# Deformable convolution, attention and experts: the first image's gather table made ahead of its offsets

## The chip, the core and the metric

The kernel runs on one core of one Trainium2 chip, in one launch. The time is device time in microseconds (us); the number that counts is the median of several runs. The profile is one further execution, recorded instruction by instruction. Engines: PE multiplies matrices (PEld loads its stationary operand), DVE is the vector engine, ACT the scalar engine, POOL (GpSimd) issues the indirect transfers, SP issues the other transfers.

## What is computed

Two layers over an image batch x of shape (4, 256, 64, 64). The change lies in the first, a modulated deformable 3x3 convolution over group-normalized x, added to x:

```python
    om = conv(gn(x), w_off) + b_off            # 27 channels: 18 offsets, 9 mask logits
    off = om[:, :2 * K2].reshape(B, K2, 2, Ho, Wo)
    mask = jax.nn.sigmoid(om[:, 2 * K2:])
    ys = off[:, :, 0] + hs[None, None, :, None] + (ki * DIL)[None, :, None, None]
    xs = off[:, :, 1] + ws[None, None, None, :] + (kj * DIL)[None, :, None, None]
    sampled = jax.vmap(_bilinear)(x, ys, xs)   # four corners, zero outside of the image
    sampled = sampled * mask[:, None]
    out = jnp.einsum('bckhw,ock->bohw', sampled, w_conv.reshape(O, C, K2))
```

The second layer is a token-wise attention between the four images (tied over positions) and a mixture of 8 experts, of which each token takes 2. Its code isn't touched, apart from the place of three small loads.

## The kernel before

**Sampling.** Each image has 32 tiles of 128 positions, and each tile 9 taps: 288 steps an image, 1152 in all, in one loop whose order of instructions on PE, DVE, ACT and POOL is written out by hand (L601 `tc.manual_schedule`); SP's order is left to a scheduler. A step gathers, for 128 positions, a row of 1024 numbers (the four corners of the tap, 256 channels each) from a table in DRAM (L519). ACT multiplies corner 0 by its weight (L535), DVE adds the other three (L543), PE transposes the sum (L557), ACT copies it out (L563), and PE multiplies it by the tap's convolution weights into an accumulator (L582). Ten gather buffers are in turn: the gather for step n + 10 waits for the last corner of step n.

**The table.** For each image b, `tables[b]` holds at each padded position two neighbouring rows' channels; a gathered row is two such entries. Its borders are zeros; `borders`-like stores (L262 to L266, five for each image) write them for all four images at the start. The inside comes from `block(q)`, eight blocks of 512 positions: `norm` makes xs, the normalized block (L353, ACT, one for each half of the channels), `turn` transposes it on PE (L363), `leave` copies it out on ACT (L372) and stores it with four transfers on SP (L378). Two zt buffers are in turn.

**The offsets.** The same `block(q)` makes the 27 offset channels from xs: `rows_of` (six products into po, L390), `shifted` (three shifted copies on ACT into oc, L402), `summed` (four small products into pt, L411), `kept` (a copy on DVE into om, L417). po, pt and the small statistics pm share two PSUM buffers (tag "om" of `ps_om`), tpx and tps the four of `ps_tp`. When all eight blocks are there, sixteen DVE operations on 576 or 288 elements a partition (L452 to L488) and a sigmoid on ACT (L447) turn om into the gather's indices idx and the corner weights wts.

**Where this stands in time.** `pieces(b)` lists all of that, with the step at which each piece is to be issued: the group statistics from step 32 (16 pieces), block q of 25 steps at 56 + 22 q, positions from step 235. For images 1 to 3 the pieces stand between the sampling steps of the image before. For image 0 there is nothing to stand between: `emit(pieces(0))` runs them at the start, in an order that the scheduler picks, and `routed` after them (L136 to L152), which multiplies the router's weights into the convolution's weights on PE and copies 18 small results on DVE. The first gather comes after all of this. `load_image(b + 1)` (L223) comes at the first step for image 1, and six steps before the end of an image for the others.

Of the kernel before, what the change touches and what calls it, by code (L numbers as in the profile page):

```python
# [9 lines left out]
F32 = mybir.dt.float32  # L10
I32 = mybir.dt.int32
AF = mybir.ActivationFunctionType
ALU = mybir.AluOpType
# [28 lines left out]
LOAD_AHEAD = 6  # L42
FIRST = 32
PERIOD = 22
NBLK = HW // BLK
# [24 lines left out]
def conv_attn_moe_kernel(  # L70
# [50 lines left out]
    def per_channel(ap, name):  # L121
# [3 lines left out]
        return t  # L125

    gamma_c = per_channel(gamma, "gamma_c")
    beta_c = per_channel(beta, "beta_c")
    bg_c = per_channel(bg, "bg_c")

# [71 lines left out]
    with ExitStack() as actx:  # L202
# [44 lines left out]

        ocs = [aw.tile([3 * QUAD, RB, W], F32, name=f"oc{n}") for n in range(2)]
        for oc in ocs:
# [6 lines left out]

        zeros = aw.tile([P, 4 * C], F32, name="zeros")
        G.memset(zeros, 0.0)
        for b in range(B):
            tv = tables[b].rearrange("(y x) (two c) -> y x two c", x=TW, two=2)  # L260
            zv = zeros.rearrange("p (a two c) -> p a two c", a=2, two=2)
            nc.sync.dma_start(tv[0, 1 : W + 1, 0, :], zeros[:W, :C])  # L262
            nc.sync.dma_start(tv[H, 1 : W + 1, 1, :], zeros[:W, :C])
            nc.sync.dma_start(tv[H + 1], zv[:TW, 0])
            nc.sync.dma_start(tv[: H + 1, 0], zv[: H + 1, 0])
            nc.sync.dma_start(tv[: H + 1, W + 1 :], zv[: H + 1])  # L266

# [16 lines left out]

        params = {}

        def pieces(b):


            out_ = []  # L290
            xr = xraw[b]
# [26 lines left out]

            n = FIRST
            for ch in range(NCH):  # L320
                for j in range(NBLK):
                    out_.append((n, lambda ch=ch, j=j: stats(ch, j)))
                    n += 1
# [11 lines left out]
            tv = tables[b].rearrange("(y x) (two c) -> y x two c", x=TW, two=2)  # L335
            om = atmp.tile([P, NR, NOFF], F32, name=f"om{b}", tag="om")

            def block(q):

                y0 = q * RB - 1  # L340
                lo, hi = max(y0, 0), min(y0 + RB + 2, H)
                t = {}

                def norm(ch):
                    if ch == 0:
                        t["xs"] = apad.tile(
                            [P, NCH, RB + 2, W], F32, name=f"xs{b}_{q}", tag="xs"
                        )
                        if lo > y0:
                            G.memset(t["xs"][:, :, 0, :], 0.0)  # L350
                        if hi < y0 + RB + 2:
                            G.memset(t["xs"][:, :, RB + 1, :], 0.0)
                    S.activation(  # L353
                        t["xs"][:, ch, lo - y0 : hi - y0], xrv[:, ch, lo:hi], AF.Identity,
                        bias=nb[:, ch : ch + 1], scale=rs[:, ch : ch + 1],
                    )

# [10 lines left out]
                def leave(i):  # L368
                    if i == 0:
                        t["zt"] = ast.tile([P, NT, C], F32, name=f"zt{b}_{q}", tag="zt")  # L370
                    zt = t["zt"]
                    S.copy(zt[:, i, :], t["tp"])  # L372
                    if i < NT - 1:
                        return
                    for yl in range(2):
                        for two in range(2):
                            yy = q * RB + yl + 1 - two
                            nc.sync.dma_start(  # L378
                                tv[yy : yy + RB - 1 : 2, 1 : W + 1, two, :].rearrange(
                                    "t x c -> x t c"  # L380
                                ),
                                zt[yl * W : (yl + 1) * W],
                            )
# [11 lines left out]

                oc = ocs[q % 2]

# [18 lines left out]
                def kept():  # L416
                    V.tensor_copy(om[:, q * NT : (q + 1) * NT, :], t["pt"])  # L417

                at = n + q * PERIOD
                out_.append((at, lambda: norm(0)))  # L420
                out_.append((at + 1, lambda: norm(1)))
                for i in range(NT):
                    out_.append((at + 3 + 4 * i, lambda i=i: turn(i)))
                    out_.append((at + 4 + 4 * i, lambda i=i: leave(i)))
                for m in range(NCH * 3):
                    out_.append((at + 4 + 2 * m + m // 2, lambda m=m: rows_of(m)))
                for kj in range(3):
                    out_.append((at + 18 + kj, lambda kj=kj: shifted(kj)))
                out_.append((at + 22, lambda: summed(0)))
                out_.append((at + 23, lambda: summed(1)))  # L430
                out_.append((at + 24, kept))

            for q in range(NBLK):
                block(q)
            n += (NBLK - 1) * PERIOD + 25

            shape = [P, 2, NR, K2]
            t = {}  # L440

            def tmp(key, tag, dtype=F32, shape=shape):
                t[key] = atmp.tile(shape, dtype, name=f"{key}{b}", tag=tag)
                return t[key]

            def masked():
                S.activation(  # L447
                    tmp("mask", "mask", shape=[P, NR, K2]), om[:, :, 2 * K2 :], AF.Sigmoid
                )

            def placed():
                V.tensor_tensor(  # L452
                    tmp("pos", "pos"),
                    om[:, :, : 2 * K2].rearrange("p r (k two) -> p two r k", two=2),
                    grid, ALU.add,
                )

            def indexed():
                p0 = t["p0"]
                params[b] = [ap_.tile([P, NR, K2], I32, name=f"idx{b}", tag="idx")]  # L460
                V.tensor_scalar(
                    p0[:, 0], p0[:, 0], float(TW), float(TW + 1), ALU.mult, ALU.add
                )
                V.tensor_tensor(params[b][0], p0[:, 0], p0[:, 1], ALU.add)

            def weighted(corner):


                if corner == 0:
                    params[b].append(  # L470
                        ap_.tile([P, 4, NR, K2], F32, name=f"wts{b}", tag="wts")
                    )
                wy, wx = (("hi", "lo")[corner % 2], ("hi", "lo")[corner // 2])
                V.tensor_tensor(params[b][1][:, corner], t[wy][:, 0], t[wx][:, 1], ALU.mult)

            def both(key):
                V.tensor_tensor(t[key][:, 0], t[key][:, 0], t["mask"], ALU.mult)

            for fn in (
                placed,  # L480
                lambda: V.tensor_tensor(t["pos"], t["pos"], taps, ALU.add),
                lambda: V.tensor_scalar(t["pos"], t["pos"], -1.0, float(H), ALU.max, ALU.min),
                lambda: V.tensor_copy(tmp("pi", "ki32", I32), t["pos"]),
                lambda: V.tensor_copy(tmp("p0", "p0"), t["pi"]),
                lambda: V.tensor_tensor(tmp("over", "over"), t["p0"], t["pos"], ALU.is_gt),
                lambda: V.tensor_tensor(t["p0"], t["p0"], t["over"], ALU.subtract),
                lambda: V.tensor_tensor(tmp("lo", "over"), t["pos"], t["p0"], ALU.subtract),
                lambda: V.tensor_scalar(  # L488
                    tmp("hi", "pos"), t["lo"], -1.0, 1.0, ALU.mult, ALU.add
                ),  # L490
                indexed,
                lambda: both("hi"),
                lambda: both("lo"),
                *(lambda c=c: weighted(c) for c in range(4)),
            ):
                out_.append((n, fn))
                n += 1
            out_.append((n - 15, masked))
            assert n <= STEPS - AHEAD, n
            return out_  # L500

        def emit(todo):
            for _, fn in sorted(todo, key=lambda p: p[0]):
                fn()
# [89 lines left out]

        emit(pieces(0))
        routed(
# [4 lines left out]
        with tc.manual_schedule(engines=order):  # L601
# [5 lines left out]
            for n in range(2):  # L607
                corners(n)
            todo = {}
            for n in range(total + 2):  # L610
                b, at = divmod(n + LOAD_AHEAD, STEPS)
                if at == 0 or n == 0:
                    if b + 1 < B:
                        load_image(b + 1)
                        for when, fn in pieces(b + 1):
                            todo.setdefault(b * STEPS + when, []).append(fn)
# [86 lines left out]

    rsum = route_pool.tile([P, NE], F32, name="rsum")

    with ExitStack() as bctx:
# [782 lines left out]
```

## Time and profile before

| what | us |
|---|---|
| median of three runs (3273.08, 3274.14, 3282.42) | 3274.14 |
| the profiled execution, time | 3278.02 |
| the profiled execution, span of its instructions | 3276.3 |
| opening, up to the first gather (L519) | 127.8 |
| sampling, first gather to the last step's products | 127.8 to 1863.7 |
| attention and experts after it | 1863.7 to 3276.3 |

Over the whole span PE is busy for 2972.6 us (91%), DVE 2600.0 (79%), POOL 1854.4 (57%), ACT 1722.3 (53%). A busy PE isn't PE at its peak, since its instructions are pipelined and their ends modelled; so the stretches count more than the sum. The granted PE clock was 0.958 over the span, 0.86 in the first 128 us.

Times of the four images, from the copy of an image's first accumulator (L591) to that of the next image's first: 152.9, 601.8, 1053.1 and 1492.7 us are the four starts; the last copy is at 1863.7.

How to read the page's lines: a group has its line, engine, operation, result<-operands, shape and count, then busy us and mean ns of one, then the idle time just before it and what ended that. A wait has who waited for whom, the sum, how often, and the longest.

### The profile page before, as it was taken

What the parts mean: (1) busy time and instruction counts of PE and PEld (TensorE: products, weight loads), DVE (VectorE), ACT (ScalarE), POOL (GpSimd) and SP (SyncE); (2) the same over time, 40 slices, a digit from 0 to 9 for tenths busy, and PEclk for the clock granted to TensorE, in tenths of its full rate; (3) what the DMA queues carried; (4) which work ended last, traced back from release to release, by engine and by line L of the source; (5) the groups of instructions that cost most, each with busy time, mean ns of one, the idle gap of its engine ahead of it and who ended that gap; (6) DMA issues with size and microseconds to landing.
All of it is one profiled execution on the core that took longest, in us unless ns stands there. A gap on an engine that the chain in (4) does not pass through costs nothing. (4 is left out here: it accounts for less than half of the span.)

```text
span 3276.3 us, 49563 instructions
## 1 busy us (share of the span) xinstructions
PE 2972.6 (91%) x13658; PEld 2175.3 (66%) x13658; DVE 2600.0 (79%) x6611; ACT 1722.3 (53%) x3912; POOL 1854.4 (57%) x1800
## 2 busy tenths in 40 slices
PE   6889998899998899989999898978888899999995
PEld 2667776677776677767777644434444488888883
DVE  1488888878897888899999788878888766567777
ACT  3456665556664566655555444334242355556552
POOL 0377667676676767677777411105676767554440
PEclk8799999999998999999999899989999999999995
DMA  5789999999999899999999821106453445447778
GB/s 167 261 330 405 390 386 345 400 340 386 390 351 393 336 402 386 386 342 409 409 404 402 312 66 55 60 24 200 156 173 104 136 137 169 159 159 248 245 236 316
DMA packets 322182, 898.89 MB, mean 274 GB/s; under 512 B 43218, under 2 KB 89949, under 8 KB 319860
## 3 DMA queue, kind: packets, MB, share of 16 engines
q0 software_dynamic: 191808, 671.74, 53.1%
q1 hardware_dynamic: 130100, 223.98, 21.1%
q8 instruction: 113, 1.85, 0.2%
q14 instruction: 161, 1.32, 0.1%
HBM read 744.43 MB, written 154.79 MB: 274 GB/s over the span
## 5 line engine op out<-in xcount | busy, mean ns | idle before, releaser
L543 DVE SCALAR_TENSOR_TENSOR s<-g,wts,s 128x256 f32<-128x256 f32 x3456 | 1446.5, 480 | 226.4 <-ACT s L535 220.2
L519 POOL DMA_INDIRECT g<-table,idx x1152 | 1220.6, 1060 | 536.7 <-DVE s L543 279.7
L582 PE MATMUL acc<-wconv_sb,sT 128*128 128x264 f32 x4608 | 1275.2, 400 | 58.6 <-ACT sT L563 57.7
L582 PEld LDWEIGHTS acc<-wconv_sb,sT 128*128 128x128 f32 x4608 | 794.2, 192 | 186.6 <-ACT sT L563 83.9
L535 ACT ACTIVATE s<-g,wts 128x256 f32<-128x256 f32 x1152 | 587.5, 510 | 342.1 <-DMA g<-table,idx 322.4
L563 ACT COPY sT<-tps 128x256 f32<-128x256 f32 x1152 | 418.8, 364 | 352.9 <-PE tps L557 347.5
L557 PE MATMUL tps<-ident,s 128*128 128x128 f32 x2304 | 449.1, 277 | 48.6 <-DVE s L543 48.0
L557 PEld LDWEIGHTS tps<-ident,s 128*128 128x128 f32 x2304 | 316.3, 144 | 260.6 <-issue 170.9
L1313 POOL DMA_INDIRECT ys_rows<-y,to x284 | 282.7, 995 | 259.6 <-DVE y L1310 191.5
L1039 POOL DMA_INDIRECT xs_rows<-u,slots x256 | 260.6, 1018 | 126.8 <-issue 110.7
L1284 PE MATMUL ph<-xT,w 128*128 128x256 f32 x1136 | 270.8, 381 | 0.7 <-ACT hT L1288 0.6
L1302 PE MATMUL py<-w,hT 128*128 128x256 f32 x1136 | 268.4, 379 | 0.0
L1288 ACT ACTIVATE hT<-ph,w 128x256 f32<-128x256 f32 x284 | 134.4, 474 | 198.0 <-PE ph L1284 197.5
L1302 PEld LDWEIGHTS py<-w,hT 128*128 128x128 f32 x1136 | 215.8, 190 | 29.3
L1307 DVE TENSOR_TENSOR y<-py,w 128x512 f32<-128x512 f32 x142 | 98.2, 692 | 171.0 <-ACT w L1246 129.8
L1284 PEld LDWEIGHTS ph<-xT,w 128*128 128x128 f32 x1136 | 206.2, 192 | 24.1 <-ACT hT L1288 1.6
L390 PE MATMUL po<-xs,woff_sb 128*96 128x512 f32 x384 | 204.3, 628 | 0.0
L176 POOL TENSOR_TENSOR l_rstd<-l_ve,nhalf 128x4 f32<-128x4 f32 x32 | 34.4, 1075 | 253.7 <-DVE l_ve L170 253.7
L881 ACT ACTIVATE gate<-pg,bg_c 128x512 f32<-128x512 f32 x64 | 43.9, 686 | 243.0 <-PE pg L686 242.9
L759 DVE SCALAR_TENSOR_TENSOR junk<-q,k 128x512 f32<-128x512 f32 x256 | 160.9, 684 | 8.9 <-ACT k L752 8.9
L876 DVE SCALAR_TENSOR_TENSOR mix<-pv,att,mix 128x512 f32<-128x512 f32 x192 | 129.7, 742 | 1.9 <-PE pv L686 1.9
L908 PE MATMUL po<-wo_sb,mix 128*128 128x264 f32 x512 | 117.8, 386 | 0.0
(228 smaller groups left out, 3287.8 us busy)
## 6 DMA issues: line engine op xcount, KB each, us to landing
xt<-xs_rows SPq DMA_DIRECT2D x142, 260.0 KB
table<-zt SPq DMA_DIRECT2D x128, 256.0 KB
early_state<-ys_rows SPq DMA_DIRECT2D x128, 256.0 KB
g<-table,idx POOLq DMA_INDIRECT x1152, 7.8
t<-o SPq DMA_DIRECT2D x32, 528.0 KB
bt<-t SPq DMA_DIRECT2D x32, 528.0 KB
dt<-t SPq DMA_DIRECT2D x64, 264.0 KB
xraw<-in_x SPq DMA_DIRECT2D x16, 1024.0 KB
```

The source lines that it names most:

```text
L390: T.matmul(t["po"], woff_sb[:, ch, ki].rearrange("p kj o -> p (kj o)"), t["xs"][:, ch, ki : ki + RB], start=(n == 0), stop=(n == NCH * 3 - 1),
L519: g = G.indirect_dma_start(out=gs[n % NGB], out_offset=None, in_=tables[b], in_offset=bass.IndirectOffsetOnAxis(ap=params[b][0][:, r, k : ...
L535: first = S.activation(ss[n], gs[n % NGB][:, :C], AF.Copy, scale=params[b][1][:, 0, r, k : k + 1])
L543: last_corner[n] = V.scalar_tensor_tensor(ss[n], gs[n % NGB][:, c * C : (c + 1) * C], params[b][1][:, c, r, k : k + 1], ss[n], ALU.mult, A ...
L557: T.transpose(tps[n][:, ch * P : (ch + 1) * P], s[:, ch * P : (ch + 1) * P], ident)
L563: S.copy(sTs[n], tps.pop(n))
L582: T.matmul(accs[n // K2][:, :CR], sT[:, ch * P : (ch + 1) * P], wconv_sb[:, ch, k, :], start=False, stop=(k == K2 - 1 and ch == NCH - 1),)
L759: V.scalar_tensor_tensor(junk, qs[s_][:, ch, :], 1.0, ks[t_][:, ch, :], ALU.mult, ALU.mult, accum_out=parts[:, ch, s_ * B + t_, j : j + 1],)
L1039: s = G.indirect_dma_start(out=rows_, out_offset=bass.IndirectOffsetOnAxis(ap=slots[:, k, n : n + 1], axis=0), in_=u[:, n % NT, :], in_off ...
L1284: T.matmul(ph, w1_sb[:, ch, f * P : (f + 1) * P], xT[:, ch, :], start=(ch == 0), stop=(ch == NCH - 1),)
L1302: T.matmul(py[:, i, :], hT[:, f, i * P : (i + 1) * P], w2_sb[:, f, :], start=(f == 0), stop=(f == NCH - 1),)
L1313: s = G.indirect_dma_start(out=ys_rows[g], out_offset=bass.IndirectOffsetOnAxis(ap=to[:, i : i + 1], axis=0), in_=y[:, i, :], in_offset=No ...
```

## The change

- Image 0's blocks come at the start without most of their offsets: all eight write the table, and only the first three (EARLY = 3) make offsets there and positions block by block. Their norms are made by DVE (`alone=True`) instead of ACT.
- Offsets and positions of blocks 3 to 7 become pieces between the sampling steps of image 0, at steps (q - 2) * 36 + 12: 48, 84, 120, 156 and 192. For these, xs is normalized a second time (ACT, a tag and buffer of its own), and oc has a third tile. Two position operations are issued in each step, on 72 or 36 elements instead of 576 or 288.
- The borders of tables 1 to 3 are stored together with the load of their image, and these loads wait for the last table store of the image before in SP's order (`issue_after`). The zero tile is half as wide; the widest border store reads it twice.
- gamma, beta and bg are loaded later.
- For images 1 to 3 the pieces are the ones of before, at the same steps.

```diff
+EARLY = 3
...
-    gamma_c = per_channel(gamma, "gamma_c")
-    beta_c = per_channel(beta, "beta_c")
-    bg_c = per_channel(bg, "bg_c")
...
-        ocs = [aw.tile([3 * QUAD, RB, W], F32, name=f"oc{n}") for n in range(2)]
+        ocs = [aw.tile([3 * QUAD, RB, W], F32, name=f"oc{n}") for n in range(3)]
...
-        for b in range(B):
+
+        def borders(b):
...
-            nc.sync.dma_start(tv[: H + 1, W + 1 :], zv[: H + 1])
+            nc.sync.dma_start(
+                tv[: H + 1, W + 1 :], zv[: H + 1].to_broadcast([H + 1, 2, 2, C])
+            )
...
-            def block(q):
-
+            def block(q, at, table=True, offsets=True, alone=False):
...
-                    S.activation(
-                        t["xs"][:, ch, lo - y0 : hi - y0], xrv[:, ch, lo:hi], AF.Identity,
-                        bias=nb[:, ch : ch + 1], scale=rs[:, ch : ch + 1],
-                    )
+                    to, of = t["xs"][:, ch, lo - y0 : hi - y0], xrv[:, ch, lo:hi]
+                    scale, bias = rs[:, ch : ch + 1], nb[:, ch : ch + 1]
+                    if alone:
+                        V.tensor_scalar(to, of, scale, bias, ALU.mult, ALU.add)
+                    else:
+                        S.activation(to, of, AF.Identity, bias=bias, scale=scale)
...
-                            nc.sync.dma_start(
+                            stores[b] = nc.sync.dma_start(
...
-                oc = ocs[q % 2]
+                oc = ocs[q % 2 if table else 2]
...
+            def positions(rows, given, at, each):
...
+                for i, fn in enumerate((
+                    placed,
+                    lambda: add(t["pos"], taps[:, :, rows]),
+                    clamp,
+                    lambda: V.tensor_copy(tmp("pi", "ki32", I32), t["pos"]),
+                    lambda: V.tensor_copy(tmp("p0", "p0"), t["pi"]),
+                    compare,
+                    lambda: V.tensor_tensor(t["p0"], t["p0"], t["over"], ALU.subtract),
+                    rest,
+                    other,
+                    indexed,
+                    lambda: both("hi"),
+                    lambda: both("lo"),
+                    *(lambda c=c: weighted(c) for c in range(4)),
+                )):
+                    done_.append((at + i // each, fn))
+                done_.append((at + 1, masked))
+                return done_
...
+            if b:
+                for q in range(NBLK):
+                    block(q, n + q * PERIOD)
...
+            place_for()
             for q in range(NBLK):
-                block(q)
...
+                early = q < EARLY
+                later_ = block(q, n + 6 * q, offsets=early, alone=True)
+                if early:
+                    later_.extend(
+                        positions(rows_in(q), lambda q=q: of[q], n + 17 * q + 25, 1)
+                    )
+                first.extend(later_)
+            for q in range(EARLY, NBLK):
+                at = (q - 2) * NT * K2 + 12
+                block(q, at, table=False)
+                later.extend(positions(rows_in(q), lambda q=q: of[q], at + 25, 2))
+                assert at + 33 <= q * NT * K2 - AHEAD, q
+            emit(first)
+            return later
...
-        emit(pieces(0))
+        borders(0)
+        todo = {}
+        for when, fn in pieces(0):
+            todo.setdefault(when, []).append(fn)
...
-                        load_image(b + 1)
+                        with tc.issue_after(stores[b].ins):
+                            load_image(b + 1)
+                            borders(b + 1)
```

## The prediction

> **What bounds the kernel now.** First the windows, to see which engine is full in which stretch (columns: stretch and its length, busy us and count of PE, PEld, DVE, ACT, POOL, granted PE clock, DMA share, GB/s).
>
> ```profile
> 30.00:80.00 50.00, 40.73 (x127) 19.23 (x125) 1.08 (x4) 21.80 (x39) 0.00 (x0) 0.83 0.45 118
> 112.00:126.00 14.00, 13.95 (x72) 13.85 (x70) 2.30 (x5) 3.72 (x10) 0.00 (x0) 0.50 0.43 173
> ...
> 251.00:497.00 246.00, 244.23 (x1290) 190.51 (x1289) 202.64 (x493) 165.79 (x410) 166.62 (x165) 1.00 1.01 393
> 1500.00:1660.00 160.00, 154.41 (x802) 122.46 (x800) 152.30 (x360) 95.91 (x253) 115.51 (x121) 1.00 1.02 408
> ```
>
> In the opening (30 to 80) nothing but PE works much. In the middle of image 0 (251 to 497), where the blocks of image 1 are made between the steps, PE is full: 244.23 of 246. In image 3, which makes no blocks (1500 to 1660), DMA and DVE are full. Then the steps in each of the two (corner 0 runs once a step):
>
> ```profile
> L535 ACT ACTIVATE s<-g,wts 128x256 f32<-128x256 f32 x162 | 82.8, 511 | 5.9 <-DMA g<-table,idx 3.4 <-DVE s L543 2.0
> L535 ACT ACTIVATE s<-g,wts 128x256 f32<-128x256 f32 x120 | 61.0, 509 | 64.4 <-DMA g<-table,idx 62.3 <-DVE s L543 2.1
> ```
>
> So 246/162 = 1.52 us a step with blocks; without them 1.28 us, the distance of two neighbouring corners in the timeline (149.66, 150.94, 152.22). Last the waits of the opening, and its timeline:
>
> ```profile
> POOL g L519 <- DVE idx L464: 39.0, 1, 39.0
> DVE wconv_sb L152 <- PE wconv_pr L147: 11.6, 1, 11.6
> PE wo_tp L143 <- DMA wo_sb<-in_wo: 2.4, 1, 2.4
> ```
>
> ```profile
> 23.29 0.16 DVE L317 SCALAR_TENSOR_TENSOR nb<-gm,rs 128x2 f32<-128x2 f32 x1 [0.84 <-POOL rs L329]
> 96.75 1.04 PE L363 MATMUL tpx<-ident,xs 128*128 128x128 f32 x8
> 99.02 1.20 ACT L372 COPY zt<-tpx 128x256 f32<-128x256 f32 x4
> 99.05 1.07 PE L411 MATMUL pt<-tap_sum,oc 96*128 96x27 f32 x8 [1.27 <-ACT oc L402]
> 99.96 5.37 PE L390 MATMUL po<-xs,woff_sb 128*96 128x512 f32 x12
> 100.25 3.43 SPq L378 DMA_DIRECT2D table<-zt  x4
> 103.73 4.43 SPq L223 DMA_DIRECT2D xraw<-in_x  x4
> 125.98 0.17 DVE L152 COPY wconv_sb<-wconv_pr 128x8 f32<-128x8 f32 x1 [11.59 <-PE wconv_pr L147]
> 127.77 1.51 POOL L519 DMA_INDIRECT g<-table,idx  x1 [38.98 <-DVE idx L464]
> ```
>
> The first gather goes at 127.77, held by the indices; the indices were held by one router copy that stood ahead of them on DVE and waited 11.59 us for PE. The table's last store was issued by 103.7.
>
> **The change, part by part.** All sums are made against the profiled execution (3278.02 us, span 3276.3). The median of the runs, 3274.14, lies 3.9 lower; I take those 3.9 off at the end.
>
> *The first gather.* It now waits for the table's last store, since only the indices of blocks 0 to 2 are made ahead of it and no router copy stands before them on DVE. When does that store land? The three per-channel loads leave the head of SP (image load at 2.32 now, at 0.80 then), so the group statistics end at 23.45 - 1.5 = 21.9. PE then has, up to the end of block 0's offsets, 18 offset products (two passes each; 12 passes 5.37, so 0.43 a pass, 0.86 a product) = 15.5, 25 transposes of 1.04/8 = 3.3, four sums 1.1: 19.9 at full clock, 24 at the 0.83 of the opening, and some 3 more for the half-rate start: 49. Block 2's offsets leave PE about 3 later: 52. Behind them DVE has 45 operations on 36 or 72 elements and six norms. The small ones aren't in the trace; neighbours are 0.16 (128x2) and 0.76 (128x576, two tensors): I take 0.23, ends 0.16 and 0.35. A norm of 128x640 with two scalars per partition isn't there either: L188, the same operation on 128x256, takes 0.409, which scales to 0.73 to 0.8 back to back; the low end is L482, 0.452 for 128x576 with constants.
>
> ```profile
> L188 DVE TENSOR_SCALAR bt<-bt,l_mv,l_rstd 128x256 f32<-128x256 f32 x20 | 7.0, 409 | 5.1 <-POOL l_rstd L176 5.1
> L482 DVE TENSOR_SCALAR pos<-pos 128x576 f32<-128x576 f32 x3 | 1.4, 452 | 0.0
> ```
>
> 45 x 0.23 + 6 x 0.73 = 14.7, so DVE is done at 67; last transposes and copies 2.2, then the stores of blocks 6 and 7 one after the other on SP, 3.43 each, 75 to 76; the stores issued from 58.74 to 62.16 kept DMA busy until 65, so landing takes 3 more: 78 at best. Two store buffers, each free only when its store has landed, can add a few us to each of the last blocks; if PE stays at half clock it is 90. I take 81, ends 78 and 92: 127.8 - 81 = **-46.8** (-50 to -36).
>
> [...]
>
> *The router products of the convolution's weights* (18 rounds of 1.17 us, 105 to 126) stay behind the last transposes on PE, from about 71 to 92 now, and DVE's first corner behind them. They hide under the gathers: see the next term. [...]
>
> *Given back at once.* Image 1's load (4 x 1024 KB) and one table's borders (652 KB) went before the first gather; now they are issued right behind the last store. 4.86 MB at the 408 GB/s of the full window are 11.9 us; some 4 pass before the first gather's packets, **+8** (+4 to +12) on gathers that pace at 1.28. Queued on SP behind them is only the first t1 store, which nobody waits for until the next phase.
>
> *Five blocks of offsets move into image 0.* Each is 6 x 0.86 + 8 x 0.13 = 6.2 us of PE. PE is full there: 162 steps x 1.11 (distance of its transposes at 143.30, 144.41 and 145.53, where data is ready) + 18 tiles x 0.6 (image and router products, 151.69 to 152.28) + 7.4 blocks x 7.2 (8 transposes, 12 passes, 8 sums) = 244, against 244.23 busy. So they cost 5 x 6.2 = 31, less some 2.5 where the first of them (steps 48 to 56) meets image 1's statistics, where PE has idle time: **+28.5** (+20 to +33). Their other engines have cover: ACT 4 us a block at 165.79 of 246 busy, DVE some 4 at 202.64 of 246. Where a norm of one chain meets a shift of the other in one step, ACT holds sT back: **+2** (0 to +6).
>
> *Borders of tables 2 and 3* (five issues each on SP, ahead of the next image's load, some 2.5 us of SP before steps that don't need that load for 30 steps) move into steps where DMA isn't the bound, 1.6 us each at 408 GB/s: **+1** (0 to +3). *The next phase:* the moved buffers let five weight loads be issued ahead of the last gathers; the 2.4 us that wo_tp waited for its load go: **-2.4** (-3 to 0).
>
> Sum: -46.8 + 8 + 28.5 + 2 + 1 - 2.4 = -9.7: 3278.0 - 9.7 = 3268.3, and 3.9 lower for the median, **3264.4**.
>
> **Rivals.** *The added blocks don't fit between the others (slower).* Both chains take po and pt from the same two PSUM buffers and pass through ACT in order. In the opening each block made PE wait 2.23 us for its shift. If each of the five blocks stops PE twice for that, and image 1's block beside it twice, 5 x 4 x 2.23 = 45 instead of the 2 taken: 3307; with half of these stops 3285. It decides from 20 us on. For it: one po of image 1 needs a buffer that is freed in the same step; against it: PE waits for almost nothing with one chain in flight. *The gather comes late (no change):* at 92 the saving is 36, the sum +1, 3275; with none of the load over before the gathers 3279. For it: DVE makes all positions of block 2 ahead of the last two norms. *PE has room (clearly faster):* then the 28.5 fall away, 3236; 244.23 of 246 speaks against it. *That the change doesn't do what it says:* if the first gather waited for all indices, nothing would be saved; in the changed program's order of instructions the first gather waits for the queue of the stores alone, and block 0's indices stand far ahead on DVE.
>
> **How the numbers follow.** About 0.3%, 9.8 us, is what a measurement of this kernel can tell from no change. The sum holds: 0.58, with 3264 as its middle and 3256 to 3274 its own range; that is at the bound, so 0.34 faster and 0.24 the same. PE has room: 0.08, faster. Late gather: 0.17, of it 0.11 the same, 0.06 slower. Blocks don't fit: 0.17, 0.13 slower, 0.04 the same. Together 0.42, 0.39, 0.19. The range: low is the gather at 78, 4 given back, 24 for the blocks, 3 from the next phase: -49.8 + 4 + 24 - 3 = -24.8, 3249; high is the late gather with one stop of 2.23 a block, 3275 + 11 = 3286.
>
> **What would show it.** First gather at 78 to 92; steps 48 to 217 of image 0 at about 1.69 us instead of 1.52 (image 0's tiles together 30 us longer), the other images unchanged to 3 us; PE at 98% there. Wrong: a gather after 95, PE under 93% in that stretch, or image 0 longer by less than 20.

## The result, and the profile after

| | before | after |
|---|---|---|
| median of 10 runs each, us | 3274.63 | 3262.86 |
| lowest and highest | 3266.56, 3290.80 | 3253.61, 3268.85 |
| profiled execution, span | 3276.3 | 3251.8 |
| first gather | 127.77 | 78.63 |
| copy of the first accumulator of image 0 | 152.9 | 113.4 |
| images 0, 1, 2, 3 (first copy to first copy, image 3 to its last) | 448.9, 451.3, 439.6, 371.0 | 474.5, 443.8, 437.6, 371.0 |
| last accumulator copy to the end | 1412.6 | 1411.6 |

The ratio after to before, taken over the runs, is 0.9954, 95% interval 0.9934 to 0.9974: 15 us faster, between 9 and 22. The two medians lie 11.8 us apart, inside that interval. The prediction was 3264.4.

First the windows of after (columns as in the prediction: busy us and counts of PE, PEld, DVE, ACT, POOL, then granted PE clock, DMA share, GB/s), and one group of the steps in the third of them:

```profile
30.00:80.00 50.00, 36.78 (x160) 26.25 (x159) 15.46 (x66) 20.81 (x51) 1.41 (x2) 0.67 0.78 191
78.60:90.00 11.40, 11.40 (x60) 11.40 (x59) 0.00 (x0) 3.80 (x10) 8.55 (x9) 0.50 1.01 406
175.00:455.00 280.00, 276.62 (x1396) 206.34 (x1395) 217.84 (x579) 183.44 (x441) 170.53 (x171) 1.00 0.95 346
1540.00:1640.00 100.00, 95.99 (x505) 76.84 (x503) 95.02 (x226) 59.99 (x159) 72.24 (x76) 1.00 1.02 405
```

```profile
L593 ACT ACTIVATE s<-g,wts 128x256 f32<-128x256 f32 x165 | 84.2, 510 | 0.6
```

In the steps that now carry two chains of blocks, PE is busy for 276.62 of 280 us, and a step takes 280/165 = 1.70 us (before: 1.52). DMA, at a share of 1.01 in the middle of image 0 before, is down to 0.95 there, so it isn't what sets the pace. Image 3 is as it was. Then the waits of the opening, and its timeline:

```profile
DVE wconv_sb L149 <- PE wconv_pr L144: 28.4, 1, 28.4
POOL g L577 <- DMA table<-zt: 16.9, 1, 16.9
ACT zt L378 <- DMA table<-zt: 6.3, 3, 2.6
```

```profile
21.49 0.16 DVE L317 SCALAR_TENSOR_TENSOR nb<-gm,rs 128x2 f32<-128x2 f32 x1 [0.84 <-POOL rs L330]
61.49 1.07 DVE L360 TENSOR_SCALAR xs<-xraw,rs,nb 128x576 f32<-128x576 f32 x2 [1.60 <-PE tpx L369]
68.82 1.20 ACT L378 COPY zt<-tpx 128x256 f32<-128x256 f32 x4 [2.38 <-DMA table<-zt]
74.50 3.53 SPq L220 DMA_DIRECT2D xraw<-in_x  x4
78.63 1.21 POOL L577 DMA_INDIRECT g<-table,idx  x1 [16.91 <-DMA table<-zt]
79.71 9.10 SPq L263 DMA_DIRECT2D table<-zeros  x1
90.98 1.41 DVE L149 COPY wconv_sb<-wconv_pr 128x8 f32<-128x8 f32 x18 [28.42 <-PE wconv_pr L144]
91.82 0.51 ACT L593 ACTIVATE s<-g,wts 128x256 f32<-128x256 f32 x1 [2.32 <-DMA g<-table,idx]
```

The last thing that the first gather waits for is the table's last store. DVE's 18 router copies now wait 28.4 us without holding the gather; they hold DVE's first corner until 92. Behind the last store stand image 1's load and a border store whose issue takes 9.10 us.

The two profiled executions lie 24.4 us apart: that of after is the fastest of its ten runs, that of before 3.4 us above its median. Summed by stretches, the profiles give -49.1 (first gather), +9.6 (from the first gather to the first accumulator copy: 34.7 us against 25.1), +25.6 (image 0), -9.5 (images 1 and 2), -1.0 (the phases behind). Images 1 and 2 run the same instructions at the same steps in both kernels, and nearly all of the -9.5 stands in one place of each, shortly after the statistics of the next image: -7.0 between the sixth and the eighth accumulator copy of image 1, -2.4 at the same copies of image 2. The timeline of POOL, image 1, before and then after:

```profile
671.61 0.22 POOL L350 MEMSET xs<- 128x128 f32 x1
672.00 7.53 POOL L519 DMA_INDIRECT g<-table,idx  x1 [0.17 <-DVE s L543]
```

```profile
657.47 0.22 POOL L354 MEMSET xs<- 128x128 f32 x1
657.86 0.95 POOL L577 DMA_INDIRECT g<-table,idx  x1 [0.17 <-issue]
```

One gather takes 7.53 us or 0.95. From the sixth to the seventh accumulator copy of image 1, where this falls, it took 18.1 us before, 13.1 after, and 13.1, 16.7, 14.5 and 14.5 in the first four runs below: it varies between executions of the same instructions. Without images 1 and 2 the change is worth 24.4 - 9.5 = 14.9 us, close to the ratio of the runs. Image 0 has the same varying place (18.9 us before, 15.4 after), so this agreement to a few tenths is in part chance.

### The profile page after: what moved, and what is told of

It reads as the page before. It is cut to its first block, busy times and chain, and to the rows that moved or that the text cites. A ratio compares the mean times of both kernels' runs of the same rounds, so it can differ in the third digit from the quotient of the medians.

```text
span 3251.8 us, 49706 instructions
## 1 busy us (share of the span) xinstructions
PE 2965.7 (91%) x13658; PEld 2178.1 (67%) x13658; DVE 2620.5 (81%) x6747; ACT 1717.1 (53%) x3913; POOL 1829.6 (56%) x1801
## 5 line engine op out<-in xcount | busy, mean ns | idle before, releaser
L577 POOL DMA_INDIRECT g<-table,idx x1152 | 1197.3, 1039 | 563.1 <-DVE s L601 330.8
L640 PE MATMUL acc<-wconv_sb,sT 128*128 128x264 f32 x4608 | 1273.3, 399 | 54.5 <-ACT sT L621 53.2
L1368 PEld LDWEIGHTS py<-w,hT 128*128 128x128 f32 x1136 | 216.1, 190 | 29.5
L1350 PEld LDWEIGHTS ph<-xT,w 128*128 128x128 f32 x1136 | 206.7, 192 | 24.4 <-ACT hT L1354 1.7
L173 POOL TENSOR_TENSOR l_rstd<-l_ve,nhalf 128x4 f32<-128x4 f32 x32 | 34.7, 1084 | 250.8 <-DVE l_ve L167 250.8
L396 PE MATMUL po<-xs,woff_sb 128*96 128x512 f32 x324 | 166.3, 598 | 0.0
```

The source lines that it names most:

```text
L396: T.matmul(t["po"], woff_sb[:, ch, ki].rearrange("p kj o -> p (kj o)"), t["xs"][:, ch, ki : ki + RB], start=(n == 0), stop=(n == NCH * 3 - 1),
L577: g = G.indirect_dma_start(out=gs[n % NGB], out_offset=None, in_=tables[b], in_offset=bass.IndirectOffsetOnAxis(ap=params[b][0][:, r, k : ...
L640: T.matmul(accs[n // K2][:, :CR], sT[:, ch * P : (ch + 1) * P], wconv_sb[:, ch, k, :], start=False, stop=(k == K2 - 1 and ch == NCH - 1),)
L1350: T.matmul(ph, w1_sb[:, ch, f * P : (f + 1) * P], xT[:, ch, :], start=(ch == 0), stop=(ch == NCH - 1),)
L1368: T.matmul(py[:, i, :], hT[:, f, i * P : (i + 1) * P], w2_sb[:, f, :], start=(f == 0), stop=(f == NCH - 1),)
```

## The experiments

e1 to e4 ran where the kernel before had a median of 3276.88, as in the result; e5 to e8 and e9 to e12 on two other chips, where it had 3620.99 and 3622.56. There the opening is the same and the sampling is slower (see e9), so of those runs the opening is compared, and whole times only as ratios to before on the same chip. The times inside a run come from one profiled execution each. "The changed kernel" is after.

**e1: all offsets ahead of the first gather.** One part alone: table first and borders later, but no block moved.

```diff
-EARLY = 3
+EARLY = 8
```

> All eight blocks make offsets ahead of the first gather (EARLY = 8); nothing stands between image 0's steps but image 1's own blocks. Theory (PE time decides): image 0 goes back from 474.5 to 449 us (+-4). In the changed kernel's opening PE idles 13 us between 40 and 70, so of the 5 x 6.2 = 31 us of PE that return there some 18 show: first gather at 97 instead of 78.6 if PE keeps its clock, up to 112 if it runs at 0.50. The whole: 8 us faster to 8 slower than the changed kernel. Rival (the blocks cost by collisions on ACT and in PSUM, more than their PE time): image 0 falls to 440 or less and the whole is over 10 us faster than the changed kernel. Rival (image 0 got longer for another reason than its blocks): image 0 stays over 465.

Measured: 3240.54 us, ratio to before 0.9899 (0.9871 to 0.9928). First gather 87.84, first accumulator copy 121.6, image 0 448.1. Image 0 fell by 26.4 as the theory had it. The opening was far cheaper than I expected: the first gather is 9.2 us later and not 18 to 33, and the whole is not level with the changed kernel but, by the two ratios, 0.9954 - 0.9899 = 0.55% or 18 us faster. In the traces it is 8.2 later at the first accumulator copy and 26.4 less in image 0, a net 18.2. The two profiled spans lie only 11.2 apart: in e1's, images 1 to 3 took 2.0 longer and the phases behind them 5.0, where the kernels don't differ. Windows of after, then of e1:

```profile
40.00:50.00 10.00, 7.81 (x44) 5.87 (x43) 3.78 (x13) 7.59 (x15) 0.00 (x0) 0.85 0.90 205
50.00:60.00 10.00, 3.44 (x15) 2.29 (x14) 9.28 (x50) 2.60 (x9) 0.00 (x0) 0.50 0.59 130
60.00:70.00 10.00, 5.53 (x23) 3.96 (x22) 1.07 (x2) 3.22 (x11) 0.20 (x1) 0.50 0.96 231
70.00:80.00 10.00, 10.00 (x52) 9.78 (x51) 0.00 (x0) 3.69 (x11) 1.21 (x1) 0.50 0.96 278
```

```profile
40.00:50.00 10.00, 9.52 (x43) 5.34 (x44) 5.98 (x28) 7.19 (x15) 0.00 (x0) 1.00 0.84 195
50.00:60.00 10.00, 10.00 (x41) 5.14 (x40) 4.93 (x21) 5.17 (x11) 0.00 (x0) 1.00 0.59 131
60.00:70.00 10.00, 10.00 (x38) 4.82 (x37) 6.34 (x34) 4.69 (x13) 0.21 (x1) 1.00 0.50 116
70.00:80.00 10.00, 10.00 (x48) 5.77 (x47) 6.30 (x36) 5.23 (x12) 0.00 (x0) 1.00 0.76 173
```

From 40 to 70 PE of the changed kernel works for 16.8 us of 30, at a clock that falls to 0.50; in e1 it works for 29.5 of 30 at 1.00. So 12.7 us of the blocks' work fill idle time; some 3 more lie behind the last transposes (those end at 78.3, the last sums at 82.8), where the first gather doesn't wait for them; and the transposes themselves run at a granted 1.00, where after's from 50 on had 0.50. How the rest divides isn't shown. Of 31 us of PE, 9 showed in the first gather where the blocks stood before, and they were moved to a place where PE is full.

**e2: two of the five blocks back.**

```diff
-EARLY = 3
+EARLY = 5
```

> EARLY = 5: the offsets of blocks 3 and 4 return to the opening, those of 5 to 7 stay between the steps. Theory: image 0 falls by 2 x 5.1 = 10.2 to 464 us; their 12.4 us of PE fit nearly into the 13 us that PE idled between 40 and 70 in the changed kernel, so the first gather comes at 79 to 87; the whole is 2 to 10 us faster than the changed kernel. Rival (the table's stores and not PE leave those 13 us, and anything put there pushes the last transposes back in full): first gather at 91, the whole 2 us slower than the changed kernel.

Measured: 3259.57 us, ratio 0.9958 (0.9941 to 0.9974); first gather 83.12, image 0 470.6. The first gather fits the theory, image 0 fell by 3.9 and not by 10.2, and the whole is that of the changed kernel. The theory took the mean of the five blocks, 5.1 us each, and they aren't equal. Windows from the 13th to the 24th accumulator copy of image 0, where blocks 5 to 7 stand: before, after, and e3 (below).

```profile
319.25:469.76 150.51, 149.36 (x788) 116.39 (x787) 124.66 (x304) 102.17 (x252) 100.38 (x101) 1.00 1.01 387
286.13:456.60 170.47, 167.66 (x848) 125.01 (x848) 130.25 (x342) 113.06 (x269) 99.05 (x101) 1.00 0.95 344
277.98:436.28 158.30, 155.32 (x818) 120.18 (x818) 129.77 (x342) 112.60 (x270) 101.45 (x101) 1.00 0.99 371
```

This stretch takes 150.5 us in before and in e1, 170.5 in after and in e2: the three blocks cost 20.0, 6.7 each, and they are still there in e2. Blocks 3 and 4 cost only 25.6 - 20.0 = 5.6 together, and with them gone 3.9 came back; the varying place, which lies among them, took 18.0 us in e2 and 15.4 in after.

**e3: what of a block costs.**

```diff
-                        start=(n == 0), stop=(n == NCH * 3 - 1),
+                        start=(n == 0), stop=(n == NCH * 3 - 1 or not table),
...
-                    for m in range(NCH * 3):
+                    for m in range(NCH * 3 if table else 1):
```

> The five blocks between image 0's steps make one product of six into po (the other five, each 0.86 us of PE, are left out, so their offsets and all that is sampled there are other values). Everything else of them stays: norms, shifts, sums, copies, positions. Theory (they cost by PE time): image 0 falls by 5 x 5 x 0.86 = 21.5, from 474.5 to 453 us. Rival (they cost by ACT's order, DVE's positions or the two PSUM buffers): it falls by 5 at most, to 469 or more. The opening stays as it is.

Measured: ratio 0.9905 (0.9881 to 0.9929); image 0 455.3, the opening unchanged (78.64, 113.2). 19.2 us went with 25 products, 0.77 each, the varying place included (13.1 us here, 15.4 in after). In the stretch of blocks 5 to 7, shown under e2, 12.2 us went with 15 products, 0.81 each. Of the 20.0 us that these blocks cost in after, 167.66 - 149.36 = 18.3 are PE's busy time and 1.7 are idle time of PE, and the idle time stays in e3 with the norms, shifts and positions. There PE waits 2.7 us for ACT's sT, in after and in e3 alike, and 0.8 in e1. So nine tenths of the price are PE's time; the collision on ACT is there too, 0.6 us a block. (The sampled positions are others in e3; whether that changes the gathers' time isn't separated.)

**e4: image 1's load at the start,** ahead of table 0's borders.

```diff
         rwc_sb = load_weight(aw, router_w, "rwc_sb")
+        load_image(1)
...
-                            load_image(b + 1)
+                            if b:
+                                load_image(b + 1)
```

> Image 1 is loaded right behind the weights at the start instead of behind the last table store; image 1's borders stay behind the store. Theory (of the 49 us that the first gather gained, 9.5 were given back to this load and the borders, 4.8 MB at 408 GB/s): the fourth accumulator copy comes at 141 instead of 148.9 us, the first gather stays within 2 us of 78.6, and the whole is 7 us faster than the changed kernel. Rival (the router products on PE at half clock and the DVE copies behind them hold the first corners until 92 anyway, and the load is hidden behind that): the fourth copy stays at 147 or later, and the whole is the same. Rival (the load, now ahead of the table's border stores, delays the opening): first gather at 84 or later.

Measured: 3267.98 us, ratio 0.9967 (0.9951 to 0.9982). The third expectation came nearest: first gather 83.89, 5.3 late. The load on DMA delays the borders (from 20 to 30 DMA is at a share of 1.05 and 410 GB/s, in after at 0.46 and 129; the issue of the border store at L263 takes 6.56 us, in after 2.04): the first table stores are issued on time, at 32.45, but ACT's copies wait 10.9 us for stores to land (after: 6.3). From there to the first accumulator copy it takes 30.3 us and not 34.7, so 4.4 of the 9.6 did come back; a gather of 5.64 us at 111.7 then lost as much. Moving a load ahead of what the end waits for is no gain.

**e5: norms on ACT again.**

```diff
-                    if alone:
+                    if alone and dve:
                         V.tensor_scalar(to, of, scale, bias, ALU.mult, ALU.add)
...
-                later_ = block(q, n + 6 * q, offsets=early, alone=True)
+                later_ = block(q, n + 6 * q, offsets=early, alone=True, dve=False)
```

> One part of the change undone: the eight norms of image 0's table blocks are made by ACT again (0.92 us each half) and not by DVE (0.61). Theory (DVE sets the table's end: in the changed kernel the last two norms stand on DVE behind the positions of blocks 1 and 2, which end at 61): with the norms off DVE the last transposes no longer wait for it, and the first gather comes at 70 to 76 instead of 78.6. Rival (ACT becomes the chain: its copies and shifts wait for PE in order and hold the norms behind them): the first gather comes at 82 to 95. Rival (the two store buffers and the landing of the stores set the end): 77 to 80, and the whole unchanged.

Measured: first gather 80.96, 2.4 later than the changed kernel's 78.5 to 78.6 (e9); ratio 0.9892 (0.985 to 0.9935), where e9 on a like chip has 0.9886. The theory fell: with the norms off DVE the end didn't come earlier, though DVE was done with the positions at 54.5. ACT's copies waited 8.9 us for the two store buffers (after: 6.3). It is nearest to the third expectation, and the move to DVE is worth some 2 us.

**e6: all borders at the start again.**

```diff
-        borders(0)
+        for b in range(B):
+            borders(b)
...
-                            borders(b + 1)
```

> One part of the change undone: the borders of all four tables are stored at the start again. Theory (late borders cost about 1 us for tables 2 and 3 together, and 1.6 of the 9.5 us given back for table 1): first gather within 2 us of 78.6, the fourth accumulator copy 1 to 2 us earlier relative to it, images 1 and 2 shorter by 0 to 1 us each; the whole within 3 us of the changed kernel. Rival (the borders in front of the table's stores on SP and in DMA delay them, and moving them is where the gain came from): first gather at 84 or later, the whole 5 us slower or more.

Measured: first gather 84.92, ratio 0.9916 (0.9892 to 0.9939). The rival was right for the opening; for the whole it isn't told apart from e9. SP of e6, and of after, at the first table stores:

```profile
37.45 1.57 SPq L263 DMA_DIRECT2D table<-zeros  x1
39.07 2.12 SPq L264 DMA_DIRECT2D table<-zeros  x1
41.84 38.69 SPq L384 DMA_DIRECT2D table<-zt  x32
```

```profile
32.30 28.64 SPq L384 DMA_DIRECT2D table<-zt  x20
```

Fifteen border stores ahead of it in SP's queue let the first table store go at 41.84 and not at 32.30; the two zt buffers make that a wait of ACT (13.1 us for stores that haven't landed, 6.3 in after) and of PE (10.8 us for ACT's copies, 5.9 in after). "Borders later" is worth 6.3 us of the first gather. Behind it nothing came back: the first corner comes 10.7 us after the first gather and the first accumulator copy 35.8 (after: 10.4 and 34.7), though no border store stands there any more. The load and the router copies are still there.

**e7 and e8: what takes 9.6 us back.** In e7 the router rounds stand among the pieces of the opening; e8 also loads image 1 behind `borders(0)`.

```diff
+            for i, w in enumerate(rows):
+                first.append((n + 24 + 2 * i, lambda i=i, w=w: routed_one(i, w)))
...
-        routed(
-            [wconv_sb[:, ch, k, :] for k in range(K2) for ch in range(NCH)], rwc_sb, ps_tp, ps_om,
-            asm, "wconv",
-        )
```

And in e8 alone:

```diff
         borders(0)
+        load_image(1)
...
-                            load_image(b + 1)
+                            if b:
+                                load_image(b + 1)
```

> The 18 rounds of router products stand among the transposes of blocks 4 to 7 on PE instead of behind them (same work, accumulated in another PSUM buffer). In the changed kernel PE idles 13 us between 40 and 70, and the rounds take 11 us at full clock, 21 at 0.50: first gather 79 to 87. What was given back is the fourth accumulator copy minus the first gather, 70.3 us against 60.7 before. Theory (the image load on DMA takes it): it stays at 69 to 71. Rival (the router products hold DVE's first corners until 92): it falls to 61 to 64.

> As e7, and image 1 is loaded at the start as well, this time behind the border stores of table 0. Theory and rival agree here: with both gone, the fourth accumulator copy comes 61 to 63 us after the first gather. The first gather is expected within 3 us of the one in e7; the fourth copy then at 140 to 149 instead of 148.9, the whole 0 to 9 us faster than the changed kernel. If the fourth copy is still 66 us or more behind the first gather, neither of the two is what takes the time back.

Measured: first gather 86.66 and 94.69, ratios 0.9893 (0.9843 to 0.9944) and 0.9905 (0.9868 to 0.9942). The expectations named the fourth copy: it came 77.3 us behind the first gather in e7 and 75.3 in e8. By the words of the second expectation (66 or more) neither part is what takes the time back. But on these chips the slower sampling shifts that copy (78.3 in e9, 70.3 in after), so the first copy is read instead, a choice made after the result: 35.1 us behind the first gather in e7, 29.5 in e8, against 34.4 in e9, 34.7 in after and 25.1 before. It varies too: 39.7 in e5, whose edit lies ahead of the first gather. Windows of e7, then of e8, from shortly before the first gather on:

```profile
84.00:88.00 4.00, 0.00 (x0) 0.00 (x0) 0.00 (x0) 0.00 (x0) 1.21 (x1) 0.50 0.97 269
88.00:92.00 4.00, 0.00 (x0) 0.00 (x0) 0.00 (x0) 0.00 (x0) 2.91 (x4) 0.50 0.98 382
92.00:96.00 4.00, 0.00 (x0) 0.00 (x0) 0.00 (x0) 0.01 (x1) 3.08 (x4) 0.50 1.01 401
```

```profile
92.00:96.00 4.00, 0.00 (x0) 0.00 (x0) 0.00 (x0) 0.00 (x0) 1.21 (x1) 0.50 0.59 134
96.00:100.00 4.00, 0.00 (x0) 0.00 (x0) 0.00 (x0) 0.00 (x0) 2.87 (x4) 0.50 0.81 191
```

In e7 PE, DVE and ACT stand idle, the router products are done, and still the first gather's data take 9.3 us while DMA is full: the load takes the time, as predicted. The rival fell for the changed kernel. In e8 the load is gone too and 5.6 us came back, as 4.4 did in e4. The 4.4 that are left (29.5 against 25.1) pass with the border stores of table 1, while DMA is at a share of 0.59 to 0.81 and 134 to 191 GB/s. That the borders are their cause is argued from these windows; no run takes load, router rounds and borders away together.

**e9: the changed kernel again.**

> The changed kernel once more, as a measure for the runs beside it. Expected: a ratio of 0.993 to 0.998, image 0 at 473 to 477 us and the other two images that make blocks at 437 to 452; first gather 78.6 and fourth accumulator copy 148.9, each within 2 us.

Measured: ratio 0.9886 (0.9814 to 0.9957), median 3575.44 beside 3622.56; the expected ratio and image times were missed. First gather 78.54, first corner 88.97, first accumulator copy 113.0 (after: 78.63, 88.99, 113.4): the opening is the same up to there (the fourth copy came at 156.8, not 148.9). The images took 511.7, 500.7, 502.4 and 492.0, all longer. The window of 100 us in image 3, to be held against 1540 to 1640 of after:

```profile
1700.00:1800.00 100.00, 78.77 (x368) 61.44 (x367) 69.44 (x167) 44.47 (x118) 67.56 (x60) 0.88 0.87 312
```

DVE makes the corners of 167/3 = 56 steps there instead of 226/3 = 75, and neither PE nor DMA is full. Half of image 3's gathers still follow each other within 1.28 us, but eleven take over 3 us, 78 us together; in after's image 3 none does. The reason stays open.

**e10: table 1's borders behind image 0's first output,** on top of e1.

```diff
                 put = nc.sync.dma_start(t1[b][r // NT], outs[b])
+                if (b, r) == (0, NT - 1):
+                    with tc.issue_after(put.ins):
+                        borders(1)
...
-                            borders(b + 1)
+                            if b:
+                                borders(b + 1)
```

> As e1 (all offsets first), with the borders of table 1 stored behind the first output of image 0 (step 37) and not ahead of the first gathers' data. In e1 the fourth accumulator copy came 69.4 us after the first gather (before: 60.7). Theory (the 652 KB of border stores, slow for their size, stand ahead of the gathers' data): 63 to 66, and the whole 3 to 6 us faster than e1. Rival (the router products behind the last offsets hold DVE until 101 in e1, whatever DMA does): 68 to 70, the whole as e1.

Measured: first gather 87.46, first accumulator copy 36.7 us behind it (e1: 33.8), ratio 0.9909 (0.9873 to 0.9944). Nothing came back: with eight blocks of offsets ahead of them DVE's router copies wait for PE until 103.5 (e1: 102.1), and the first corners stand behind them whatever DMA does. The rival was right. On these two chips e1's gain isn't seen: image 0 takes 508.8 to 512.3 us without the five blocks between its steps (e10 to e12) and 507.3 to 520.9 with them (e5 to e9), and e10's ratio is no better than e9's. PE is busy for 263.79 us of 280 in e9 where it was for 276.62 in after (175 to 455), so it has room for them there.

**e11: the blocks in series,** on top of e1.

```diff
-                later_ = block(q, n + 6 * q, offsets=early, alone=True)
+                later_ = block(q, n + 22 * q, offsets=early, alone=True)
...
-                        positions(rows_in(q), lambda q=q: of[q], n + 17 * q + 25, 1)
+                        positions(rows_in(q), lambda q=q: of[q], n + 22 * q + 25, 1)
```

> As e1 (all offsets first, norms on DVE), with the eight blocks 22 places apart in the list as in the kernel before, and not 6. Theory (blocks that overlap keep PE busy while one of them waits for its shifts on ACT; in the kernel before each shift cost PE 2.23 us): PE idles again, the last transposes come 15 to 20 us later, and the first gather is at 100 to 110 instead of 87.8. Rival (the norms' move from ACT to DVE is what filled PE): the first gather stays at 86 to 93.

Measured: first gather 96.68, between the two expectations; first corner 117.87, ratio 0.9961 (0.9919 to 1.0003). From 40 to 70 PE works for 25.1 us of 30 (e1: 29.5). One of the waits of e11's opening:

```profile
PE pt L417 <- ACT oc L408: 10.1, 8, 1.3
```

Each of the eight blocks stops PE once, for 1.3 us, until its shifts are there. Overlap of the blocks is worth 8.8 us of the first gather.

**e12: what the runs suggested, together.**

In words, since the edit is long: all eight blocks' offsets in the opening, 8 places behind their block's transposes; three xs buffers, and four zt buffers that the outputs share; the router rounds among the last offsets, as in e7; a quarter of image 1's load behind the stores of each of blocks 2 to 5; the borders of table 1 as in e10.

> A version from the runs so far: all offsets first, but 8 places behind their block's transposes (three xs buffers), four store buffers instead of two, the router rounds among the last offsets, image 1 loaded in four parts between the table's stores, table 1's borders behind the first output of image 0. Expected if the opening is PE's work and what stands in DMA ahead of the gathers: first gather 76 to 84, first corner 4 to 7 us behind it or at the end of the router products (about 95), fourth accumulator copy at 143 to 151 against 157.2 in e1, the whole 6 to 14 us faster than e1, ratio 0.985 to 0.989. If the four parts of the load hold the table's stores back (as the load at the start did in e4), the first gather comes after 88 and nothing is won.

Measured: ratio 0.9927 (0.9898 to 0.9957), so the hoped-for gain over e1 was missed. The first gather came at 79.76, as expected and with all eight blocks' offsets in the opening, but the first corner at 105.3 and the first accumulator copy at 129.3 (e1: 121.6). POOL, and DVE's router copies:

```profile
91.26 0.94 POOL L616 DMA_INDIRECT g<-table,idx  x1 [0.31 <-issue]
111.76 0.94 POOL L616 DMA_INDIRECT g<-table,idx  x1 [19.55 <-DVE s L640]
```

```profile
103.55 1.41 DVE L594 COPY wconv_sb<-wconv_pr 128x8 f32<-128x8 f32 x18 [2.29 <-PE wconv_pr L584]
```

Ten gathers fill the ten buffers by 92; then POOL waits 19.55 us, since PE's router rounds end at 103 and DVE has the router copies and the last block's positions ahead of its first corner. An early gather wins nothing while PE's list isn't done.

The fastest version found is e1, on the one chip where it ran; on the other two no version was told apart from the changed kernel.

## Why the prediction was right

*The first gather* (-46.8, measured -49.1). The picture held: indices long there, the table's last store the last wait, its issue done at 74.5 (75 to 76 predicted), landed 4.2 later. Two sizes in it were wrong and evened out, which is luck. The norms take 0.53 to 0.61 us on DVE (0.73 taken), and DVE was done at 62.6 and not at 67. Of the two rows that I scaled to 640 elements, L482 (0.452 for 576, so 0.50) lay nearer than L188, from which the 0.73 came. And ACT's copies waited 6.3 us for the two store buffers, which I had put at "a few us"; the last copies, at 68.82, wait for a buffer and not for DVE. In e5, with the norms off DVE, the end didn't come earlier. My 90 "if PE stays at half clock" was wrong: PE had 0.50 from 50 on, and little was left on it by then. Undone one at a time, the parts of this gain are worth 9.2 (five blocks moved, e1), 8.8 (overlap of the blocks, e11 against e1), 6.3 (borders, e6) and 2.4 us (norms, e5). The rest of the 49.1 I put down to the order, a gather that waits for neither all indices nor the router copies; no run undid that alone.

*Given back* (+8, measured 9.6). The load in front of the gathers is shown: without it 4.4 (e4) and 5.6 us (e8) came back, one execution each. Table 1's borders were taken by their bytes, 652 KB or 1.6 us at 408 GB/s; with the load gone 4.4 us pass with them in e8, and in e6, which has the load and no borders there, nothing came back. So their share in the changed kernel stays open. The router products hide behind the load; in e1, where their first products start at 82.67, they hold DVE's first corner.

*Five blocks* (+28.5 and +2, measured 25.6, and 26.4 by e1). The mechanism is right: 276.62 of 280 us, steps of 1.70 (1.69 predicted). For blocks 5 to 7 the sizes are right too, collisions included: 3 x (6.2 + 0.4) = 19.8 predicted, 20.0 measured. What was too large is the price of blocks 3 and 4, some 10.7 predicted and 5.6 measured. They stand where PE has more idle time than the 2.5 I took off: from the 1st to the 13th accumulator copy it idles for 12.1 us before and 8.0 after. The varying place is in that stretch as well (18.9 us before, 15.4 after), so what part of it is filled idle time, and what part chance, stays open. The rival of blocks that don't fit is refuted by PE's idle time, 3.4 of 280 us. Its 2.23 us a stop was also misread: PE's eight waits for shifts in the opening before took 13.2 in all, 1.65 each, and 2.2 is the longest. The rival of room on PE is refuted by the windows.

*Borders of tables 2 and 3* (+1). Too small to see beside the place that varies by 5 us. By it image 1 came out 7.5 shorter, where I had said unchanged to 3. What I left out is that all late borders clear SP's queue ahead of the first table store: 6.3 us by e6, which my 81 held without naming it.

*The next phase* (-2.4). The wait of wo_tp is gone; its first product of pq comes 12.7 us after the last accumulator copy and not 14.8: -2.1, of which 1.0 is left at the end.

The sum with the measured terms: -49.1 + 9.6 + 25.6 - 1.0 = -14.9, against -9.7 predicted, -15 by the ratio of the runs and -11.8 by their medians. What no step of the prediction asked is what the five blocks cost where they stood. I summed them into the opening as if it were one thing; e1 shows that, where before is as fast as in the result, the change is a gain of 33 us (0.9899) with a loss of 18 built in.

## What to carry to other kernels

Work that is moved costs what its new place charges, and saves what its old place charged, which need not be its duration: 31 us of PE cost 9 us where PE idled between waits, and 26 where PE was full; on the chips where PE had room there, too little to be told. So price a move twice, and split a change that does two things before judging it. When one wait is taken away, count what stands next to it: here a load held the first steps, with it gone the border stores seemed to, and with all offsets made first the router rounds did.

## What was not expected of the hardware

The granted PE clock did not follow the busy share. In e7 PE was busy for 9.62 us of 10 between 50 and 60 at 0.56, with the router's 8-column products among transposes; in e11 for 25.1 of 30 at 0.95, with the 512-column products; in after's router rounds for 11.40 of 11.40 at 0.50, with PEld as full. In e1's router rounds PE is shown busy without a gap (16.00 of 16.00 us from 84 to 100) at 0.50, after 1.00 from 70 to 80. What sets the granted clock is not shown; no run tests it.

The kernel before had a median of 3277 us on one chip and 3621 and 3623 on two others. The changed kernel's opening, in the profile of the result (where before had 3275) and on the last of these, was the same to 0.5 us. So a profile from one chip doesn't give another's whole time.
